# A decoder layer on one core: queries and keys stored in the layout of their products, and row additions moved off GpSimd

## The chip, the cores and the metric

The kernel runs on one core of a Trainium2 chip. The time is the device time of one execution in microseconds; the kernel before has a median of 1358.45 us over three runs (1357.38 to 1362.58). A profile of one further execution is the source of everything said about single instructions.

TensorE (PE) multiplies matrices, VectorE (DVE), ScalarE (ACT) and GpSimd (POOL) work on elements, and SyncE (SP) only issues transfers here. Each engine works through its own instructions in order and waits at the head of its queue when something is not ready.

## The reference

Four sequences of 1024 tokens with 256 features go through one decoder layer, with 64 context tokens for each sequence:

```python
x = x + attention(layernorm(x), W_qkv, b_qkv, W_out, b_out)   # 16 heads of 16, softmax(q k^T) / sqrt(256)
x = x + cross_attention(layernorm(x), ctx)                    # 16 heads of 16, 64 keys
x = x + ffn(layernorm(x))   # ternary W_fc to 1024, gelu, layernorm with w and b, ternary W_proj back
```

Everything is float32. Each of the three terms ends in a sum over features that is added to the rows of `x`; the attention's outputs have a bias row each (`b_out`, called `bo` in the kernel, and the cross attention's `xbo`), and the last layer norm's offset `ln_b` multiplied with `W_proj` gives another constant row, `yrow`.

## The kernel before

**Units.** Self-attention is worked in 16 units `u`, each one batch and four heads (`g`), all 1024 queries by 1024 keys. The queries and keys are kept as the sum of a high and a low part so that products in the faster float format lose nothing: `project(b, c)` computes, for one batch and eight heads at a time (128 padded features, 16 for each head), the high part on ScalarE and the low part on VectorE (tile `hl`, two parts by 512 tokens; the two lines that write `hl` are L369 and L370). It does so for the first half of the queries, both halves of the keys, then the second half of the queries: four pieces. Each piece is stored to DRAM (`kept_q`, `kept_k`, L375) by one transfer of 512 KB. Most transfers go through the helper at L62 on SP's queue; in the very first group three of the stores go on ScalarE's.

**Fetch.** `fetch(u)` reads the four heads of a unit back, two heads ("pair") to a tile of 128 partitions: for each head 16 rows of the queries' parts in the order high, high, low, low, and of the keys' parts in the order high, low, high, low. One product over these 64 rows then gives the sum of all four part products. Since DRAM holds each part once, a tile takes eight transfers of 16 rows: 64 KB each, and for unit 0, which is fetched by halves of the tokens, 32 KB each. Half of unit 0's key fetches are issued by ScalarE (L393). The fetches of unit u+1 are issued in the first two steps of unit u.

**A unit.** `maxima(u)` multiplies queries by keys in blocks of 128 queries by 512 keys and takes the exact row maxima on VectorE (L446); the maxima are negated and split in parts as well (`nm`, L455; `nm_s`, L458 and L459), turned (`mT`, L464), and used in the scores, which are computed again with keys on the partitions; ScalarE takes the exponentials (L911), and the weighted values are summed in `ps_acc`. A unit has 16 steps (two halves of the queries by eight blocks of keys). The maxima of unit u+1 run between the scores of unit u; for unit 0 the first 32 of them must come before anything else.

**What fills the gaps.** All other work (layer norm and projections of the next batches, values, `post(b)`) is written as generators on three lines (`due`, `later`, `aside`), and a step of a unit takes pieces from them as their due times demand. The order of TensorE's instructions and of the transfers on SP is the order written in the program. On VectorE, ScalarE and GpSimd a scheduler decides the order, save for some pinned layer norm instructions. A transfer also waits for the one eight transfers before it.

**post(b).** After a batch's attention: add the bias row `bo` to `x` (four additions of 128x512 a batch on GpSimd through `add_row`, L287 to L293), output projection added to `x` (L327), layer norm (`ln_stats` L241 and L242, `ln_normalised`: one instruction for each 256-feature row block, on ScalarE at L258 in the main part and on VectorE at L265 in the last stage), then add `xbo` to `x`, turn the normalised rows (`ln_transposed`, L279 and L281), and the cross attention. `post(3)` runs in the last stage.

**The last stage** is the feed-forward part, in eight half batches. `widen(i)` normalises, turns, multiplies to 1024 features, applies gelu and takes the statistics of the last layer norm; it also adds `yrow` to `x`. `narrow(i)` turns the 1024 features, scales them (L1060, and the low part `hl` on VectorE, L1061), multiplies back to 256, adds to `x` (L1077) and stores the output. A written order interleaves the `widen` and `narrow` of neighbouring halves, and puts pieces of `post(3)` between them. `state["split"]` is true in the main part and false here.

Of the kernel before, what the change touches and what calls it, by code (L numbers as in the profile page):

```python
# [30 lines left out]
def decoder_layer(ctx, tc, a, out):  # L31
# [240 lines left out]
    def ln_transposed(dst, xn, rest=None):  # L272

        def copy(tokens, r, sides, v):
            to = of_side(dst[:, :, tokens], r, sides)
            nc.scalar.copy(to, v)  # L279
            if rest is not None:  # L280
                nc.vector.tensor_tensor(  # L281
                    of_side(rest[:, :, tokens], r, sides), v, to.bitcast(F32), ALU.subtract
                )

        turned_tokens(copy, lambda c, k: xn[:, k, c * P : (c + 1) * P], xn.shape[1])

    def add_row(t, row, n=2):  # L287

        for t in range(t, t + n, 2):
            nc.gpsimd.tensor_tensor(  # L290
                xs(t, 2), xs(t, 2),
                row.rearrange("p (o d) -> p o d", o=1).to_broadcast([P, 2, E]), ALU.add,
            )  # L293
# [56 lines left out]

    def project(b, c):

        split_of[b, c] = [
            dram.tile([2, P, S], F32, tag=f"kept_{name}", name=f"kept_{name}", bufs=6) for name in "qk"
        ]
        first = (b, c) == (0, 0)

        for side, half in ((0, 0), (1, 0), (1, 1), (0, 1)):
            w, bias = (wq, wk)[side], bqk[("bq", "bk")[side]][:, c : c + 1]
            hl = main.tile([P, 2, 512], F32, tag="exp" if first and half else "hl", name="hl", bufs=4 if first and half else 2)  # L360
            width = 256 if state["split"] else 512
            for i0 in range(0, 512, width):
                yield "cols+"
                cols, part = slice(half * 512 + i0, half * 512 + i0 + width), slice(i0, i0 + width)
                pq = bank()[:, 0:width]
                product(
                    pq, [(w[:, i, c * P : (c + 1) * P], xnT_of[b][:, i, cols]) for i in range(2)]
                )
                nc.scalar.activation(hl[:, 0, part].bitcast(F32R), pq, AF.Identity, bias=bias)  # L369
                nc.vector.scalar_tensor_tensor(  # L370
                    hl[:, 1, part], pq, bias, hl[:, 0, part], ALU.add, ALU.subtract
                )
            cols = slice(half * 512, (half + 1) * 512)
            issue = nc.scalar.dma_start if first and (side or half) else dma
            issue(out=split_of[b, c][side][:, :, cols].rearrange("l p t -> p l t"), in_=hl)  # L375
            pieces_of[b, c] = pieces_of.get((b, c), 0) + 1

    def fetch(u):

        b, g = divmod(u, NG)  # L380
        pairs = qk_of[u] = []
        rest = []
        for pair in range(2):
            q = main.tile([P, S], F32R, tag="q", name="q", bufs=4)
            k = main.tile([P, S], F32R, tag="k", name="k", bufs=4)
            pairs.append((q, k))
            kept_q, kept_k = split_of[b, g // 2]
            f0 = 64 * (g % 2) + 32 * pair

            def parts(t, kept, order, n, cols, issue, f0=f0):  # L390
                for i, part in enumerate(order):
                    r, f = 64 * n + 16 * i, f0 + 16 * n
                    issue(out=t[r : r + 16, cols].bitcast(F32), in_=kept[part, f : f + 16, cols])  # L393

            if u:
                halves = (slice(0, S),)
            else:
                halves = (slice(0, 512), slice(512, S))
            for n in range(2):
                parts(q, kept_q, (0, 0, 1, 1), n, halves[0], dma)  # L400
            for cols in halves:
                for n in range(2):
                    parts(k, kept_k, (0, 1, 0, 1), n, cols, dma if u or n else nc.scalar.dma_start)
            for n in range(2):
                for cols in halves[1:]:
                    rest.append((parts, q, kept_q, (0, 0, 1, 1), n, cols, dma))
            if pair:
                for f, *args in rest:
                    f(*args)
            yield  # L410

    def values(b):
# [140 lines left out]
    def post(b):  # L553
        t0 = b * NT
        pairs = att_of.pop(b)
        yield "free"
        add_row(t0, bo, NT)

        def projected(src, w, first, n):

            for i in range(0, n, 4):
# [17 lines left out]
        for half in range(2):  # L579
# [1 line left out]
            xnT = post_pool.tile([P, 2, 512], F32, tag="xn2T", name="xn2T")  # L581
            yield "free"
            xn = ln_normalised(post_pool, mv, rs, h0, t0 + h0, 4)
            add_row(t0 + h0, xbo, 4)
            yield "rows"
            ln_transposed(xnT, xn)
            q2 = post_pool.tile([P, 2, 512], F32, tag="q2", name="q2")
            m = 256 if state["split"] else 512
            for i in range(0, 512, m):
# [324 lines left out]
    for u in range(NU):  # L914
        b, g = divmod(u, NG)
        due.end = aside.end = 2 * NT * NG * (b + 1)
        later.end = due.end - 2
        if b % 2 and g == 0:
            due.end = 2 * NT * (u + 1)
        if g == 0:  # L920
            if b == 0:
                later.add(context(), 6)
                later.add(value_bias(), 1)

            for n in ((1, 2), (), (3,), ())[b]:
                if n > 2:
                    load_x(n)
                due.add(ln1(n), 2)
                due.add(project(n, 0), 8)
                due.add(values(n), 8)  # L930
                if n == 1:
                    due.add(project(n, 1), 8)
            if b % 2:

                due.add(project(b // 2 + 2, 1), 8)
            if b == B - 1:
                load_x(0, view=x_kept, slot=1)
        if g == 1 and b == B - 1:
            aside.add(ternary("wfc", 2, HID), 10)
            aside.add(ternary("wproj", HID // P, E), 10)  # L940
            aside.add(bias_row(), 2)
        for step in range(2 * NT):
            half, kb = divmod(step, NT)
            if u == 1 and step == 2:
                load_x(2)
            if step < 2 and 0 < u < NU - 1:
                if step == 0:
                    while pieces_of.get(divmod((u + 1) // 2, NG // 2)) != 4:
                        due.step()
                    fetching = fetch(u + 1)  # L950
                next(fetching)
            next(loading, None)
            due.grow(2 * NT * u + step)
            later.grow(2 * NT * u + step)
            aside.grow(2 * NT * u + step)
            exps = [scores(u, half, kb, 0)]
            top()
            behind = 1 if later.credit >= 1.5 else 0
            if turning and begun[turning[0]] < slots[0]:
                fill("rows", behind)  # L960
                run(turning.popleft())
            elif urgent:
                fill("rows", behind)
                urgent.popleft()()
            else:
                fill("rows", 1)
            exps.append(scores(u, half, kb, 1))

            for _ in range(2 if u == 0 and step < 3 else 1):
                top()  # L970
            if pending is not None:
                if pending[2] == 0:
                    acc = ps["acc"]()
                weigh(*pending, acc)
            fill("cols", 2)
            pending = (u, half, kb, exps)
        if g == NG - 1:

            due.flush()
            aside.flush()  # L980
            later.flush()
    weigh(*pending, acc)
    while urgent:
        urgent.popleft()()
# [16 lines left out]
    def widen(i):  # L1001
# [3 lines left out]
        for t in range(0, NH, 2):  # L1005
            cols = slice(t * P, (t + 2) * P)
            xn = ln_normalised(ffn, mv3, rs3, t0 + t, t0 + t, 2)
            ln_transposed(xh[:, :, cols], xn, rest=xl[:, :, cols])
            add_row(t0 + t, yrow)
            if t == 0:  # L1010
                yield ""
        h = ffn.tile([P, NH, HID], F32, tag="h", name="h", bufs=2)
# [32 lines left out]
    def narrow(i):  # L1045
# [6 lines left out]
        for c in range(HID // P + 2):  # L1052
# [10 lines left out]
            if c >= 2:  # L1063
                for k, part in enumerate(parts[c - 2]):
                    for n in range(NH):


                        matmul(
                            py[:, n // 2, n % 2 * E : (n % 2 + 1) * E], lhsT=part[:, n * P : (n + 1) * P],
                            rhs=wproj[:, c - 2, :], start=c == 2 and k == 0 and n % 2 == 0,  # L1070
                            stop=c == HID // P + 1 and k == 1 and n % 2 == 1,
                        )
            if 0 < c < HID // P + 1:
                yield ""
        for n in range(2):
# [113 lines left out]
```

## Time and profile before

| | |
|---|---|
| median of the runs | 1358.45 us (1357.38 to 1362.58) |
| profiled execution | 1359.89 us, its span 1358.1 us |
| TensorE busy | 1282.7 us (94%) |
| VectorE busy | 1005.3 us (74%) |
| ScalarE busy | 896.6 us (66%) |
| GpSimd busy | 79.6 us (6%) |
| mean granted TensorE clock | 0.978 |
| HBM read / written | 46.81 MB / 24.12 MB |
| 240 + 240 fetches of 64 KB | issued on SP from 48.74 us on |
| 32 + 32 fetches of 32 KB | unit 0, 16 of them issued by ScalarE |
| 32 stores of 512 KB | 29 on SP, 3 on ScalarE |
| row additions on GpSimd, 128x512 | 16 `bo`, 16 `xbo`, 16 `yrow`, about 1.3 us each |

Times in the profile are microseconds from the start of the span unless marked ns. A row of a timeline has the start, the length, the engine, the line of the kernel, the operation, what it writes and reads, and how many such instructions stand in a row; in brackets how long the engine had been idle and what ended that. SPq and ACTq are the issuing of transfers by SP and ScalarE; an issue is short, and where a row of several is long, the engine stands in them waiting. PEld is TensorE's loading of weights, which overlaps its products. PEclk is the clock that TensorE was granted, as a share of full speed. DMA share is the mean busy share of the core's 16 transfer engines.

### The profile page before, as it was taken

What the parts mean: (1) busy time and instruction counts of PE and PEld (TensorE: products, weight loads), DVE (VectorE), ACT (ScalarE), POOL (GpSimd) and SP (SyncE); (2) the same over time, 40 slices, a digit from 0 to 9 for tenths busy, and PEclk for the clock granted to TensorE, in tenths of its full rate; (3) what the DMA queues carried; (4) which work ended last, traced back from release to release, by engine and by line L of the source; (5) the groups of instructions that cost most, each with busy time, mean ns of one, the idle gap of its engine ahead of it and who ended that gap; (6) DMA issues with size and microseconds to landing.
All of it is one profiled execution on the core that took longest, in us unless ns stands there. A gap on an engine that the chain in (4) does not pass through costs nothing.

```text
span 1358.1 us, 27680 instructions
## 1 busy us (share of the span) xinstructions
PE 1282.7 (94%) x11000; PEld 719.2 (53%) x11000; DVE 1005.3 (74%) x2110; ACT 896.6 (66%) x1654; POOL 79.6 (6%) x86
## 2 busy tenths in 40 slices
PE   5889999999999999989999999999999988999987
PEld 2345445545554554444545545545455466776777
DVE  4788877767878877778877767878889357565665
ACT  1277676766677667777676676686766747474765
POOL 4000000022010000011000000010000012000000
PEclk9689999999999999999999999999999989999989
DMA  5431321302020201221111102212210010100000
GB/s 171 133 120 48 109 62 65 95 32 79 33 79 1 63 27 38 71 56 43 53 46 50 45 19 83 75 61 65 63 33 1 2 63 0 51 12 32 1 32 31
DMA packets 46576, 72.72 MB, mean 54 GB/s; under 512 B 11536, under 2 KB 28176, under 8 KB 46448
## 3 DMA queue, kind: packets, MB, share of 16 engines
q1 hardware_dynamic: 44976, 68.47, 16.7%
q10 hardware_dynamic: 1328, 2.10, 0.5%
q8 instruction: 87, 1.43, 0.4%
q0 software_dynamic: 144, 0.39, 0.2%
q14 instruction: 41, 0.34, 0.1%
HBM read 46.81 MB, written 24.12 MB: 52 GB/s over the span
## 4 chain that ended last, share of the span: by engine, by line
PE 75%; DVE 15%; ACT 7%; DMA 2%; issue 1%; SPq 0%; DVEq 0%; ACTq 0%
PE ps_ring L57 44%; PE ps_acc L57 15%; PE ps_wide L57 8%; DVE mx L446 7%; PE ps_misc L57 3%; PE ps_misc L60 2%; ACT exp L911 2%; PE ps_ring L60 2%; DVE nm L605 2%; ACT xn L258 1%; DMA x<-in_x 1%; DVE bn L241 1%; DVE xn L265 1%; DMA q<-kept_q 1%; ACT ex L638 1%
## 5 line engine op out<-in xcount | busy, mean ns | idle before, releaser
L446 DVE TENSOR_REDUCE mx<-ps_ring 128x1 f32<-128x512 f32 x1024 | 646.7, 681 | 154.7 <-PE ps_ring L57 153.7
L911 ACT ACTIVATE exp<-ps_ring 128x512 f32<-128x512 f32 x1024 | 549.3, 607 | 182.6 <-PE ps_ring L57 179.1
L57 PE MATMUL ps_ring<-q,k 64*128 64x512 f32 x1024 | 280.4, 474 | 8.3 <-ACT exp L911 5.9
L57 PE MATMUL ps_ring<-k,q 64*128 64x512 f32 x1024 | 265.3, 428 | 15.6 <-DMA k<-kept_k 4.7
L57 PE MATMUL ps_acc<-exp,v_sb 128*32 128x512 f32 x2048 | 274.5, 608 | 0.0
L57 PE MATMUL ps_ring<-mT,sel 64*128 64x512 f32 x1024 | 233.1, 401 | 0.2 <-ACT mT L464 0.2
L57 PEld LDWEIGHTS ps_ring<-q,k 64*128 64x128 f32 x1024 | 115.9, 185 | 199.0 <-ACT exp L911 68.2
L57 PEld LDWEIGHTS ps_ring<-k,q 64*128 64x128 f32 x1024 | 126.1, 187 | 98.5 <-ACT exp L911 40.9
L57 PEld LDWEIGHTS ps_ring<-mT,sel 64*128 64x128 f32 x1024 | 108.4, 187 | 6.2 <-ACT mT L464 0.7
L57 PEld LDWEIGHTS ps_acc<-exp,v_sb 128*32 128x32 f32 x2048 | 40.5, 108 | 67.2 <-issue 65.4
L1029 DVE BATCH_NORM_STATS2 bnh<-h 128x6 f32<-128x512 f32 x64 | 41.1, 679 | 34.1 <-ACT h L1026 34.0
L1026 ACT ACTIVATE h<-ps_wide 128x1024 f32<-128x1024 f32 x32 | 32.7, 1025 | 42.0 <-PE ps_wide L57 41.9
L1061 DVE SCALAR_TENSOR_TENSOR hl<-ps_misc,lnw,hT 128x512 fp32r<-128x512 f32 x64 | 46.4, 733 | 18.2 <-ACT hT L1060 18.2
L57 PE MATMUL ps_wide<-wfc,xl 128*128 128x512 f32 x128 | 56.6, 443 | 1.9 <-DVE xl L281 1.8
L57 PE MATMUL ps_wide<-wproj,hl 128*128 128x256 f32 x256 | 46.2, 303 | 12.5 <-DVE hl L1061 12.4
L57 PE MATMUL ps_wide<-wfc,xh 128*128 128x512 f32 x128 | 54.2, 423 | 0.0
L1060 ACT ACTIVATE hT<-ps_misc,lnw 128x512 fp32r<-128x512 f32 x64 | 42.6, 686 | 16.3 <-PE ps_misc L60 16.3
L241 DVE BATCH_NORM_STATS2 bn<-x 128x6 f32<-128x256 f32 x96 | 38.9, 416 | 6.6 <-DMA x<-in_x 5.0
L57 PEld LDWEIGHTS ps_wide<-wproj,hl 128*128 128x128 f32 x256 | 34.9, 192 | 16.2 <-DVE hl L1061 14.7
L290 POOL TENSOR_TENSOR x<-x,xbo 128x512 f32<-128x512 f32 x16 | 20.5, 1288 | 367.3 <-ACT xn L258 358.2
L57 PE MATMUL ps_wide<-wproj,hT 128*128 128x256 f32 x256 | 41.4, 285 | 0.0
L60 PE MATMUL ps_misc<-ident,h 128*128 128x128 f32 x256 | 37.4, 274 | 1.0 <-ACT ex L638 0.7
(166 smaller groups left out, 1436.8 us busy)
## 6 DMA issues: line engine op xcount, KB each, us to landing
q<-kept_q SPq DMA_DIRECT2D x240, 64.0 KB
k<-kept_k SPq DMA_DIRECT2D x240, 64.0 KB
kept_q<-hl SPq DMA_DIRECT2D x15, 512.0 KB
kept_k<-hl SPq DMA_DIRECT2D x14, 512.0 KB
out<-x SPq DMA_DIRECT2D x16, 256.0 KB
x<-in_x SPq DMA_DIRECT2D x3, 1024.0 KB
x_kept<-x SPq DMA_DIRECT2D x3, 1024.0 KB
x<-x_kept SPq DMA_DIRECT2D x3, 1024.0 KB
```

The lines of the kernel that those rows point to most:

```text
L57: ordered(nc.tensor.matmul(*args, **kwargs))
L60: ordered(nc.tensor.transpose(*args))
L241: pinned(nc.vector.bn_stats(out=st, in_=xs(t)[:, 0, :]))
L258: nc.scalar.activation(xn[:, k, :], xs(t + k)[:, 0, :], AF.Identity, bias=nmr[:, k : k + 1], scale=rs[:, i + k : i + k + 1],)
L290: nc.gpsimd.tensor_tensor(xs(t, 2), xs(t, 2), row.rearrange("p (o d) -> p o d", o=1).to_broadcast([P, 2, E]), ALU.add,)
L446: nc.vector.tensor_reduce(mx[:, t, 2 * pair + n : 2 * pair + n + 1, kh], pm, AX.X, ALU.max)
L605: nc.vector.tensor_reduce(nm[:, t, s, :], pm[s].rearrange("p (h k) -> p h k", k=SK), AX.X, ALU.max, negate=True,)
L911: nc.scalar.activation(ex[:, n, :], pe[n], AF.Exp)
L1026: nc.scalar.activation(h[:, t, :], ph.rearrange("p a f -> p (a f)"), AF.Gelu)
L1029: nc.vector.bn_stats(out=st[:, half, :], in_=h[:, t, half * 512 : (half + 1) * 512])
L1060: nc.scalar.activation(hT, pt, AF.Copy, scale=w)
L1061: nc.vector.scalar_tensor_tensor(hl, pt, w, hT.bitcast(F32), ALU.mult, ALU.subtract)
```

## The change

- The kept tiles get the shape [8 heads, 4 parts, 16 features, 1024 tokens], with the parts in the order in which the products take them: each part is in DRAM twice. A piece is stored by four transfers of 256 KB, one for each of the four part positions.
- A tile of a pair is then a contiguous block of 128 rows and is fetched by one transfer of 512 KB; in unit 0 by two of 256 KB (the second half of the queries after everything else, as before). All fetches are issued on SP. SP issues 245 transfers instead of 618, ScalarE 12 instead of 19.
- `bo` is added in the ninth of the sixteen steps of a batch's last unit (for batch 0, after that unit) instead of at the head of `post`, whose first yield goes.
- `xbo` is added after the normalised rows have been turned instead of before.
- `yrow` is added in `narrow`, with its columns 4 and 6, instead of in `widen`.
- `add_row` uses VectorE in the last stage: that takes the 16 `yrow` additions and the four `xbo` additions of batch 3 there. The other 28 stay on GpSimd.

The scheduler's order of VectorE and ScalarE moves with this. Of these moves three bear on what follows: the first `bn_stats` of batch 1's layer norm stands right behind the first `nm`, ahead of `nm_s`; batch 1's normalisations stand singly among the exponentials; and the statistics of batch 2 stand earlier among the maxima.

```diff
     def add_row(t, row, n=2):
 
+        engine = nc.gpsimd if state["split"] else nc.vector
         for t in range(t, t + n, 2):
-            nc.gpsimd.tensor_tensor(
+            engine.tensor_tensor(
                 xs(t, 2), xs(t, 2),
                 row.rearrange("p (o d) -> p o d", o=1).to_broadcast([P, 2, E]), ALU.add,
             )
...
         split_of[b, c] = [
-            dram.tile([2, P, S], F32, tag=f"kept_{name}", name=f"kept_{name}", bufs=6) for name in "qk"
+            dram.tile([8, 4, D, S], F32, tag=f"kept_{name}", name=f"kept_{name}", bufs=6)
+            for name in "qk"
         ]
...
             issue = nc.scalar.dma_start if first and (side or half) else dma
-            issue(out=split_of[b, c][side][:, :, cols].rearrange("l p t -> p l t"), in_=hl)
+            for i, part in enumerate(((0, 0, 1, 1), (0, 1, 0, 1))[side]):
+                issue(out=split_of[b, c][side][:, i, :, cols], in_=hl[:, part, :])
...
-            kept_q, kept_k = split_of[b, g // 2]
-            f0 = 64 * (g % 2) + 32 * pair
-
-            def parts(t, kept, order, n, cols, issue, f0=f0):
-                for i, part in enumerate(order):
-                    r, f = 64 * n + 16 * i, f0 + 16 * n
-                    issue(out=t[r : r + 16, cols].bitcast(F32), in_=kept[part, f : f + 16, cols])
...
+            h = 4 * (g % 2) + 2 * pair
+            kept_q, kept_k = (
+                t[h : h + 2].rearrange("h i f t -> (h i f) t") for t in split_of[b, g // 2]
+            )
+            halves = (slice(0, 512), slice(512, S)) if u == 0 else (slice(0, S),)
+            dma(out=q[:, halves[0]].bitcast(F32), in_=kept_q[:, halves[0]])
             for cols in halves:
-                for n in range(2):
-                    parts(k, kept_k, (0, 1, 0, 1), n, cols, dma if u or n else nc.scalar.dma_start)
+                dma(out=k[:, cols].bitcast(F32), in_=kept_k[:, cols])
+            if u == 0:
+                rest.append((q, kept_q))
             if pair:
+                for q, kept_q in rest:
+                    dma(out=q[:, 512:S].bitcast(F32), in_=kept_q[:, 512:S])
             yield
...
     def post(b):
         t0 = b * NT
         pairs = att_of.pop(b)
-        yield "free"
-        add_row(t0, bo, NT)
...
             xn = ln_normalised(post_pool, mv, rs, h0, t0 + h0, 4)
-            add_row(t0 + h0, xbo, 4)
             yield "rows"
             ln_transposed(xnT, xn)
+            add_row(t0 + h0, xbo, 4)
...
             next(loading, None)
+            if b and g == NG - 1 and step == NT:
+
+                add_row(b * NT, bo, NT)
...
             later.flush()
+            if b == 0:
+
+                add_row(0, bo, NT)
...
             ln_transposed(xh[:, :, cols], xn, rest=xl[:, :, cols])
-            add_row(t0 + t, yrow)
...
+            if c in (4, 6):
+                add_row(t0 + c - 4, yrow)
             if 0 < c < HID // P + 1:
                 yield ""
```

## The prediction

> **What bounds the kernel now.** I read the page's busy line, slices and chain first, then the issues of SP and ACT in the opening, then stretches of 10 us, and the last stage's groups at the end.
>
> ```profile
> PE 1282.7 (94%) x11000; PEld 719.2 (53%) x11000; DVE 1005.3 (74%) x2110; ACT 896.6 (66%) x1654; POOL 79.6 (6%) x86
> PE   5889999999999999989999999999999988999987
> PEclk9689999999999999999999999999999989999989
> PE 75%; DVE 15%; ACT 7%; DMA 2%; issue 1%; SPq 0%; DVEq 0%; ACTq 0%
> ```
>
> TensorE is the bound at 94%, so a gain can only come from the 75 us in which it is idle, or runs at a lower clock. The slices place them: the first three, a dip in the middle (560 to 600 us), and the last eight (the last stage, from 1095 us). From 107 to 200 us TensorE is busy 92.36 of 93.00 us, so transfers made cheaper there are worth nothing.
>
> SP's issues, then ACT's, in the opening (start, length, engine, line, what it writes and reads, count, idle before):
>
> ```profile
> 17.06 0.37 SPq L63 DMA_DIRECT2D kept_q<-hl  x1
> 19.86 6.98 SPq L63 DMA_DIRECT2D q<-kept_q  x8
> 27.62 4.68 SPq L63 DMA_DIRECT2D k<-kept_k  x8
> 48.74 5.64 SPq L63 DMA_DIRECT2D q<-kept_q  x8
> 65.53 0.42 SPq L63 DMA_DIRECT2D x<-in_x  x1
> ```
>
> ```profile
> 26.90 5.12 ACTq L393 DMA_DIRECT2D k<-kept_k  x6
> 29.65 5.93 ACTq L393 DMA_DIRECT2D k<-kept_k  x11
> 35.68 0.84 ACT L369 ACTIVATE hl<-ps_ring,bq_c 128x256 fp32r<-128x256 f32 x2 [10.82 <-DMA k<-kept_k]
> ```
>
> A store of 512 KB is issued at 17.06 and its reader at 19.86: 2.8 us. Then some 0.45 us goes for each small fetch, and ACT issues fetches until 35.6 while its `hl` work, which holds PSUM banks, stands behind them. The first row maximum starts at 31.80, the 32nd ends at 60.24, the scores start at 61.0. The next batch's x load is issued last, at 65.53.
>
> The stretches (length, PE, PEld, DVE, ACT, POOL busy with counts, granted clock, DMA share, GB/s):
>
> ```profile
> 17.00:20.00 3.00, 2.13 (x12) 1.33 (x11) 0.79 (x2) 1.65 (x3) 3.00 (x4) 1.00 0.54 211
> 50.00:60.00 10.00, 7.09 (x74) 2.98 (x66) 10.00 (x18) 1.49 (x4) 0.00 (x0) 0.97 0.61 175
> 80.00:90.00 10.00, 7.33 (x72) 3.49 (x71) 8.71 (x29) 5.62 (x11) 0.52 (x3) 1.00 0.36 113
> 90.00:100.00 10.00, 7.73 (x42) 3.33 (x44) 6.94 (x15) 9.64 (x19) 0.99 (x6) 0.66 0.00 0
> ```
>
> From 50 to 60 DVE is full: maxima at some 0.61 us each are that stage's floor. From 80 to 100 TensorE is idle 4.9 us and the clock falls to 0.66, about 2 us more: the layer norm of batch 1 stands in ACT's and DVE's way in one block. That block costs 7 us.
>
> **The opening: the transfers.** Removed: 16 fetches of 32 KB from ACT, and on SP eight issues a tensor become one (two or three halves in unit 0). Added: each store becomes four of 256 KB, 1 MB a piece for 512 KB, since every part is stored twice. Only unit 0 feels the fetches, which elsewhere land under a full TensorE.
>
> What such a store costs no row shows, because its DRAM side is now `[8,16,512]` (heads, features, tokens), where the old one began with 128. By the row, 512 KB moved in 1.35 us (18.0 to 19.4 us, 389 GB/s over 16 DMA engines, 24.3 GB/s each), so a doubled piece would take 2.7 us. The Trainium skill, "DMA: Bandwidth & Descriptors", section "Why a DMA increments its semaphore by 16 and not by 1", says that a DMA runs on the largest number of engines up to 16 that divides the slowest dimension of both sides: here 8, always the lowest-numbered. Then each 256 KB takes 1.35 us on eight engines and a piece 5.4 us, fourfold. No run here shows it. I take the rule, since nothing in the row has an outer dimension of 8, and keep the row's value for the low end.
>
> By the rule, on engines 0 to 7 (24.3 GB/s each): they start at 17.45; unit 0's four pieces 4 × 5.4 = 21.6; its eight fetches of 256 KB at 0.68, 5.4; two pieces of the next four groups 10.8; unit 1's fetches of 2 MB, 5.4; the x load of 1 MB, 2.7. Sum 45.9, plus some 1.5 us idle while SP waits for a store: x lands at about 65.5. The first keys' fetch, behind stores of the two queues, lands at 31.4, so the first maximum starts where it did; ACT now waits for store lanes till about 34 instead of 35.6. From the second keys' fetch (37.4) DVE runs on: 24 × 0.61 = 14.6, plus `hl` work, and the 32nd maximum ends at about 53.
>
> Then comes what is late next. In the built order of DVE, the first `bn` of batch 1's layer norm stands directly between `nm` and the `nm_s` that the scores need. It waits for x. Behind it are `nm_s`, the transposes, `mT`, every exp. So DVE stands from 53 to 65.5 and scores start at about 66.5, against 61.0: +5.5 us.
>
> In return, the block at 80 to 100 is gone: statistics follow at 66 (eight pairs at some 0.4 and 0.1 us), and ACT's eight normalisations stand singly among the exps. What remains: two table loads of 1.28 us on ACT and 3.3 us on DVE, side by side, at the start of scores; I take 2 left of 7: −5. (Batch 2's norm, spread in this way, lies between 107 and 200 us, where TensorE idled 0.6 us in all.)
>
> By the row's 2.7 us a piece the same sum ends otherwise: first maximum at 28, no pause before it, 32nd at 50, x landed at 48: scores at 51, −10, and the norm −3.5.
>
> **The steady part.** `hl` has two buffers; a piece written before the second-last one's stores are read would hold ACT and its exps. Stores are issued at 129.34, 146.82 and 149.15: two back is 19.8 us, against about 7.5 for four issues and 5.4 of data, so nothing. Batch 2's statistics are hoisted from 159 to some 141 us, about when its x lands: the load moves up from 146.3 to 132, behind 2 MB of fetches: 5.4, then 2.7 us: +1. The x load of batch 3, before 571.57 to 577.86 among small fetches (TensorE idle 4.7 us around it), comes through sooner: −1.5. The bo rows move from the head of `post` to a point before it and stay on POOL: 16 × 1.29 beside a full TensorE, 0; nothing else waits in POOL's queue there, and the 12 xbo rows left on it have until the projection after them. With its yield gone `post` starts one fill earlier, which moves work and adds none.
>
> **The last stage.** Four xbo and 16 yrow additions go from POOL to DVE, set right behind the normalisations by the built order. These groups (busy, mean ns, idle before) and one stretch tell the price, then DVE's own timeline:
>
> ```profile
> L290 POOL TENSOR_TENSOR x<-x,yrow 128x512 f32<-128x512 f32 x16 | 20.8, 1302 | 213.3 <-DVE xn L265 142.2 <-issue 68.5 <-DVE rsh L248 2.3
> L1077 DVE TENSOR_TENSOR x<-x,ps_wide 128x512 f32<-128x512 f32 x16 | 10.3, 682 | 9.9 <-PE ps_wide L57 9.9
> ```
>
> ```profile
> 1120.00:1140.00 20.00, 14.99 (x84) 12.55 (x83) 19.31 (x43) 13.53 (x16) 7.28 (x6) 0.95 0.00 0
> ```
>
> ```profile
> 1131.53 3.94 DVE L265 TENSOR_SCALAR xn<-x,mv,rs 128x256 f32<-128x256 f32 x6
> ```
>
> Added: 20 × 0.68 (nearest row: same shape, one side in PSUM) = 13.6 us of DVE. Removed: DVE's normalisations take 0.38 us alone and about 0.35 pipelined, but six took 3.94 us beside POOL's additions; that is 1.85 too much, and with five other such places (0.9, 1.0, 1.1, 1.0, 1.0) about 7 us goes. DVE is the bound only from 1120 to 1140 (19.31 of 20): six additions 4.1, less 2.85 relief, +1.2. In the other stretches it idles 25 to 45% and TensorE is busy; 14 additions 9.5 less 4.1, mostly hidden: +0.8. Together +2. Bounds: −7 (relief felt, additions hidden) to +10.8 (all additions felt, relief only in that stretch).
>
> **Sum.** +5.5 − 5 + 1 − 1.5 + 2 = +2 on the profiled 1359.89 (span 1358.1): 1361.9. The median of the runs, 1358.45, is 1.4 below the profiled one, so 1360.5; I say 1360.
>
> **Rivals.**
> - *Stores run on 16 engines* (the row holds, or contention is less). For it: 389 GB/s in the trace. Against: the rule. −10 − 3.5 + 1 − 1.5 + 2 = −12: 1346.
> - *The last stage decides, slower.* The additions stand ahead of `hl` or `xl`, for which TensorE already waits 12.4 us at `hl`: 10.8 in place of 2: 1369. It decides from seven uncovered additions more than I count (7 × 0.68 = 4.8). Against: DVE idles a third of most stretches.
> - *x is later or the norm isn't absorbed.* If the start costs 5.5 and the norm saves only 2, 1363.5.
> - *The transfers don't matter*: opening as before, hidden by DVE's maxima; 1358.45 + 1.5 = 1360. Only the traces tell it from my case.
>
> **How the numbers follow.** Mine 0.55; sixteen engines 0.13; last stage 0.15; norm not absorbed 0.12; transfers hidden 0.05. A measurement here tells from no change about 0.5%: 1351.7 to 1365.2. Faster: 0.12 from sixteen engines, 0.07 from mine (relief, or less waiting for x): 0.19. Slower: 0.15, 0.05 of the norm's, and 0.12 of mine (terms of 5 us each, all rough): 0.32. Within: 0.49. The range reaches to both: 1346 to 1370; mine alone 1353 to 1367.
>
> **What would show it.** Right: kept stores that land some 1.35 us after one another with DMA share near 0.5; DVE waiting about 10 us for x's load ahead of `nm_s`; scores from 66 us; no block at 80 to 100; normalisations at 0.38 us and DVE above 75% in the last stage. Wrong: share near 1 during stores, scores at about 51; or TensorE waiting for `hl` much over 12.4 us in the last stage.

## The result, and the profile after

The changed kernel takes 1374.24 us (median of six runs, 1373.14 to 1377.56) against 1360.73 us of the kernel before in the same comparison: a ratio of 1.0105, with a 95% interval of 1.0086 to 1.0124. It is slower by 13.5 us, and lies 4 us above the upper end of the predicted range. The profiled execution has a span of 1372.5 us, 14.4 more than the one before.

The page of the changed kernel, its busy line, slices and chain:

```profile
PE 1280.1 (93%) x11000; PEld 714.2 (52%) x11000; DVE 1012.7 (74%) x2130; ACT 896.9 (65%) x1654; POOL 53.4 (4%) x66
PE   4689899989999999989999999998999998999988
PEclk9789999999999999999999999999999999999999
PE 40%; DVE 10%; ACT 4%; DMA 1%; issue 1%; SPq 0%; DVEq 0%; ACTq 0%
```

TensorE's work is the same to 0.2%; its idle time has grown by 17 us (92.4 against 75.4), and the slices show that most of this lies in the first tenth of the span. Sums over the whole span don't say more. What does is to find the same instruction in both traces and take the difference of its starts. The exponentials (1024 of them, in the same order in both) and the additions of the last stage serve as marks; a change of the shift between two marks is what that stretch gained or lost:

| mark | before, us | after, us | shift | the stretch lost (+) or gained (−) | predicted |
|---|---|---|---|---|---|
| exponential 1 | 63.7 | 75.8 | +12.1 | opening +12.1 | +5.5 |
| 33 | 100.4 | 108.6 | +8.2 | layer norm of batch 1 −3.9 | −5 |
| 97 | 160.8 | 179.4 | +18.6 | layer norm of batch 2 +10.4 | +1 |
| 257 | 317.2 | 337.3 | +20.1 | +1.5: −3.6 up to exponential 221, then a jump of +5.5 at 300 us | 0 |
| 545 | 608.9 | 625.4 | +16.5 | around batch 3's x load −3.6 | −1.5 |
| 833 | 908.0 | 924.1 | +16.1 | −0.4 | 0 |
| 865 | 939.5 | 962.2 | +22.7 | ternary weights +6.6 | none |
| 993 | 1067.7 | 1091.4 | +23.7 | +1.0 | 0 |
| addition 15 of 16 at the end (`x<-x,ps_wide`) | 1353.3 | 1367.9 | +14.6 | last stage −9.1 | +2 |

SP's and ACT's timelines of the changed kernel in the opening:

```profile
16.73 3.40 SPq L63 DMA_DIRECT2D kept_q<-hl  x4
28.76 0.35 SPq L63 DMA_DIRECT2D q<-kept_q  x1
32.88 8.53 SPq L63 DMA_DIRECT2D k<-kept_k  x2
61.70 0.43 SPq L63 DMA_DIRECT2D x<-in_x  x1
```

```profile
19.54 6.38 ACTq L379 DMA_DIRECT2D kept_k<-hl  x4
25.96 0.58 ACT L279 COPY xnT<-ps_ring 128x512 f32<-128x512 f32 x1 [5.97 <-issue]
30.42 0.69 ACT L372 ACTIVATE hl<-ps_ring,bk_c 128x512 fp32r<-128x512 f32 x1 [3.87 <-PE ps_ring L57]
```

Between the first store's issue and the fetch that reads it lie 12.0 us; before it was 2.8. And ScalarE stands in its four stores for 6.4 us with the second half of the turned rows behind them, so that the second half of the keys comes 9.4 us later (30.42; before, 21.00). The first maximum starts at 40.81 instead of 31.80 (before, then after):

```profile
31.80 0.69 DVE L446 TENSOR_REDUCE mx<-ps_ring 128x1 f32<-128x512 f32 x1 [6.15 <-PE ps_ring L57]
```

```profile
40.81 1.29 DVE L440 TENSOR_REDUCE mx<-ps_ring 128x1 f32<-128x512 f32 x2 [4.29 <-PE ps_ring L57]
```

DVE's timeline behind the 32 maxima:

```profile
64.95 0.19 DVE L449 TENSOR_REDUCE nm<-mx 128x16 f32<-128x32 f32 x1
72.05 0.43 DVE L241 BATCH_NORM_STATS2 bn<-x 128x6 f32<-128x256 f32 x1 [6.91 <-DMA x<-in_x]
72.40 0.16 DVE L452 CAST nm_s<-nm 128x16 fp32r<-128x16 f32 x1
...
155.58 0.43 DVE L241 BATCH_NORM_STATS2 bn<-x 128x6 f32<-128x256 f32 x1 [6.73 <-DMA x<-in_x]
```

The wait of the prediction is there, ahead of `nm_s`, and it comes a second time for batch 2. Two more waits for late transfers follow, on ScalarE for stores of `hl` and on DVE for a load (timelines of each):

```profile
299.09 0.47 ACT L372 ACTIVATE hl<-ps_ring,bq_c 128x256 fp32r<-128x256 f32 x1 [4.02 <-DMA kept_k<-hl]
```

```profile
940.01 0.69 DVE L742 TENSOR_REDUCE part<-raw 128x1 f32<-128x512 f32 x1 [5.90 <-DMA raw<-in_wfc]
```

Each of the last three (batch 2, 300 us and 940 us) costs more than TensorE's idle time. TensorE stood for 5.81, 3.98 and 3.95 us, and its granted clock was then 0.50 for about 5 us more after it had work again, which takes some 2.4 us of work each time. Together that comes near the losses of 10.4, 5.5 and 6.6 us in the table. The stall of batch 2, and the stretches behind the stall at 300 us (the third column from the end is the clock):

```profile
156.44 0.79 PE L57 MATMUL ps_ring<-k,q 64*128 64x512 f32 x1 [5.81 <-DVE hl L373]
```

```profile
302.00:304.00 2.00, 2.00 (x20) 0.59 (x12) 0.22 (x1) 0.00 (x0) 0.00 (x0) 0.50 0.00 0
306.00:308.00 2.00, 2.00 (x24) 0.86 (x25) 2.00 (x4) 1.86 (x5) 0.00 (x0) 1.00 0.43 79
```

What the stores do to the transfer engines shows in stretches of the changed kernel (the last two columns are the DMA share and GB/s):

```profile
17.00:30.00 13.00, 6.06 (x15) 2.79 (x14) 3.41 (x12) 1.75 (x3) 3.98 (x5) 0.80 0.55 165
56.00:60.00 4.00, 3.87 (x42) 1.58 (x40) 4.00 (x7) 0.74 (x2) 0.00 (x0) 1.00 0.55 206
64.00:72.00 8.00, 0.00 (x0) 0.00 (x0) 1.10 (x3) 0.00 (x0) 0.00 (x0) 0.61 0.83 309
```

While only stores run (56 to 60), the share is about a half at 206 GB/s. From 64 to 72 TensorE does nothing at all.

The last stage, by groups of DVE instructions (the normalisations before, then two groups of the changed kernel):

```profile
L265 DVE TENSOR_SCALAR xn<-x,mv,rs 128x256 f32<-128x256 f32 x40 | 20.2, 548 | 2.6 <-PE ps_misc L60 2.0 <-PE ps_acc L57 0.6
```

```profile
L265 DVE TENSOR_SCALAR xn<-x,mv,rs 128x256 f32<-128x256 f32 x40 | 14.8, 406 | 0.6 <-PE ps_acc L57 0.6
L291 DVE TENSOR_TENSOR x<-x,yrow 128x512 f32<-128x512 f32 x16 | 10.6, 683 | 0.0
```

An addition costs 0.68 us on DVE, as the nearest row had it, and the normalisations have come down from 548 to 406 ns on average.

### The profile page after: what moved, and what is told of

It is laid out like the page before. It is cut to its first block, busy times and chain, and to the rows that moved or that the text cites. A ratio compares the mean times of both kernels' runs of the same rounds, so it can differ in the third digit from the quotient of the medians.

```text
span 1372.5 us, 27267 instructions
## 1 busy us (share of the span) xinstructions
PE 1280.1 (93%) x11000; PEld 714.2 (52%) x11000; DVE 1012.7 (74%) x2130; ACT 896.9 (65%) x1654; POOL 53.4 (4%) x66
## 4 chain that ended last, share of the span: by engine, by line
PE 40%; DVE 10%; ACT 4%; DMA 1%; issue 1%; SPq 0%; DVEq 0%; ACTq 0%
PE ps_ring L57 18%; PE ps_wide L57 8%; PE ps_acc L57 7%; DVE mx L440 4%; PE ps_misc L57 3%; PE ps_misc L60 2%; DVE nm L596 2%; ACT exp L902 1%; PE ps_ring L60 1%; DMA raw<-in_wproj 1%; DMA raw<-in_wfc 1%; DVE h L1033 0%; DVE xl L281 0%; ACT xn L258 0%; DVE hl L1057 0%
## 5 line engine op out<-in xcount | busy, mean ns | idle before, releaser
L57 PEld LDWEIGHTS ps_ring<-k,q 64*128 64x128 f32 x1024 | 123.2, 187 | 107.5 <-ACT exp L902 47.1
L57 PE MATMUL ps_wide<-wproj,hl 128*128 128x256 f32 x256 | 46.8, 306 | 10.6 <-DVE hl L1057 10.5
L57 PE MATMUL ps_ring<-xnT,wk 128*32 128x256 f32 (+1 forms) x456 | 36.7, 398 | 6.9 <-ACT xnT L279 6.9
L373 DVE SCALAR_TENSOR_TENSOR hl<-ps_ring,bq_c,hl 128x256 f32<-128x256 f32 (+1 forms) x30 | 14.9, 500 | 37.8 <-ACT hl L372 37.8
L57 PEld LDWEIGHTS ps_wide<-wproj,hl 128*128 128x128 f32 x256 | 35.3, 194 | 14.3 <-DVE hl L1057 12.6
L372 ACT ACTIVATE hl<-ps_ring,bq_c 128x256 fp32r<-128x256 f32 (+1 forms) x30 | 14.7, 495 | 42.2 <-PE ps_ring L57 33.0
```

The lines of the kernel that those rows point to most:

```text
L57: ordered(nc.tensor.matmul(*args, **kwargs))
L373: nc.vector.scalar_tensor_tensor(hl[:, 1, part], pq, bias, hl[:, 0, part], ALU.add, ALU.subtract)
```

## The experiments

Twelve kernels were run. Each ratio is against runs of the kernel before on the same chip. These kernels ran on three chips: the kernel before took 1359.68 us beside the `only` kernels and `rows16_adds`, 1361.15 beside the `early` and `once` kernels and 1360.51 beside the last four. A difference of a few microseconds between kernels of two groups is better read from the ratios.

| kernel | us | ratio (95%) |
|---|---|---|
| stores on 8 engines, additions of the change (the changed kernel) | 1374.24 | 1.0105 (1.0086 to 1.0124) |
| `dma8_only`: its transfers, additions as before | 1382.64 | 1.0170 (1.0149 to 1.0191) |
| `adds_only`: its additions, transfers as before | 1354.45 | 0.9958 (0.9942 to 0.9975) |
| `rows16_adds`: other row order, additions of the change | 1342.18 | 0.9874 (0.9853 to 0.9896) |
| `rows16_only`: other row order, additions as before | 1351.39 | 0.9932 (0.9914 to 0.9949) |
| `early_8`: the changed kernel, `x` loaded before the stores | 1367.81 | 1.0052 (1.0038 to 1.0067) |
| `early_16`: `rows16_adds`, `x` loaded before the stores | 1340.11 | 0.9844 (0.9825 to 0.9863) |
| `once`: each part stored once and read twice, additions of the change | 1336.51 | 0.9821 (0.9800 to 0.9842) |
| `once_early`: the same, `x` loaded before the stores | 1335.84 | 0.9817 (0.9801 to 0.9833) |
| `four_engines`: the changed kernel, each store cut in two | 1405.36 | 1.0330 (1.0311 to 1.0349) |
| `dve_rows`: the kernel before, its last-stage additions on DVE | 1355.75 | 0.9967 (0.9955 to 0.9980) |
| `moved_rows`: the kernel before, its additions moved, all on GpSimd | 1359.79 | 1.0000 (0.9991 to 1.0008) |
| `no_rows`: `adds_only` without the 20 additions of the last stage | 1352.56 | 0.9944 (0.9931 to 0.9956) |

### How many engines a store takes

The theory is that the store is slow because its DRAM side begins with a dimension of 8; the rivals are that the doubled bytes are the cost, or the order of the layer norm's instructions. A product over 64 rows doesn't care about the order of the rows, as long as queries and keys agree. So the row order head, feature, part, token serves as well as head, part, feature, token; with it a store is 128 rows at one stride, and nothing else changes:

```diff
-            dram.tile([8, 4, D, S], F32, tag=f"kept_{name}", name=f"kept_{name}", bufs=6)
+            dram.tile([8, D, 4, S], F32, tag=f"kept_{name}", name=f"kept_{name}", bufs=6)
...
-                issue(out=split_of[b, c][side][:, i, :, cols], in_=hl[:, part, :])
+                issue(
+                    out=split_of[b, c][side][:, :, i, cols].rearrange("h f t -> (h f) t"), in_=hl[:, part, :]
+                )
...
-                t[h : h + 2].rearrange("h i f t -> (h i f) t") for t in split_of[b, g // 2]
+                t[h : h + 2].rearrange("h f i t -> (h f i) t") for t in split_of[b, g // 2]
```

> The changed kernel, but with DRAM rows ordered head, feature, part, token, so that a store's DRAM side is 128 rows with one stride, as its SBUF side is; bytes, number of transfers and everything else stay. If the eight engines are the cause: 16 completions a store instead of 8, DMA share near 1 while stores run, about 0.65 us for 256 KB instead of 1.29, scores from about 51 us instead of 73, DVE's waits for the x loads of 6.9 and 6.7 us and ScalarE's wait of 4.0 us for a kept store gone, and a time of about 1338 us. If the doubled bytes are the cause, whatever engines carry them, some 1365 to 1374. If the order of the layer norm's instructions is the cause, 1365 to 1374 as well, with DVE still waiting ahead of nm_s.

It took 1342.18 us: 32 us less than the changed kernel, with the same bytes and the same number of transfers. The stretch of the opening, of this kernel:

```profile
17.00:30.00 13.00, 9.67 (x74) 4.70 (x76) 4.70 (x14) 3.59 (x6) 3.35 (x5) 0.87 0.97 305
```

The share is 0.97 where it was 0.55. All 2130 instructions of DVE stand in the changed kernel's order, with the first `bn` between `nm` and `nm_s`, so the order alone is not the cause. But the waits for x are shorter rather than gone (2.14 us ahead of `nm_s`, 2.30 us at batch 2): scores start at 55.8, not at 51, and the two waits together are about the 4 us by which it missed 1338.

> The change's stores and fetches alone; all row additions where the kernel before has them, on GpSimd. If the last stage gained from the additions (the shift between the traces falls from 23.7 to 14.6 us there), this is about 9 us slower than the changed kernel, near 1383 us. If the last stage's gain is only slack taken up again after a late start, it is as the changed kernel, 1374.

> Stores and fetches with rows ordered head, feature, part, token, row additions as before. If the engines and the additions are two separate effects: about 9 us above the run that has both, near 1347 us. If the transfers' gain is given back in the last stage, nearer to 1360.

> The row additions alone; stores and fetches as before. If the additions gain 9 us in the last stage: about 1351 us. As I had predicted for the last stage (+2): 1362. If the gain is slack: 1360.

These three, with `rows16_adds`, the changed kernel and the one before, take the two halves of the change apart. `dma8_only` came out as expected; `adds_only` and `rows16_only` each took some 4 us longer than expected, but nearer to that than to the other case. With the additions as before, the eight-engine stores cost 23.0 us (1382.64 − 1359.68) and the sixteen-engine stores gain 8.3. The additions gain 5.2 us beside the old stores and 9.2 beside the sixteen-engine ones; beside the eight-engine ones the two medians differ by 8.4. They are not slack taken up again: they gain without any late start. By the marks the last stage itself gains 8.8 us in `adds_only`, 9.0 in `rows16_adds` and 9.1 in the changed kernel; `adds_only` gains less in all because it is 2.2 us behind the kernel before when the last stage begins. Nor does the last stage gain from the transfers beside the sixteen-engine stores (−0.1 in `rows16_only`); in `dma8_only` it takes back 2.7 us.

The other direction of the same cause is a store cut in two, of four heads each, with twice as many transfers:

```diff
-                issue(out=split_of[b, c][side][:, i, :, cols], in_=hl[:, part, :])
+                for h in (0, 4):
+                    issue(
+                        out=split_of[b, c][side][h : h + 4, i, :, cols],
+                        in_=hl[16 * h : 16 * h + 64, part, :],
+                    )
```

> The changed kernel with each store cut into two of four heads, so that the slowest dimension of the DRAM side is 4. By the rule: four completions a store, 128 KB in about 1.29 us, a piece 10.3 us, DMA share near 0.25 while only stores run; with six pieces ahead of batch 1's x it lands near 95 us, scores start about 20 us later than in the changed kernel, and the time is 1395 us or more. If the number of engines follows from the bytes or the partitions, 1374 to 1380.

1405.36 us. A stretch of this kernel in which only stores run:

```profile
28.00:32.00 4.00, 0.00 (x0) 0.00 (x0) 0.00 (x0) 0.00 (x0) 0.00 (x0) 0.50 0.26 102
```

The share is a quarter. The trace also records the completions of each transfer, one for every engine that took part. Set side by side, with the time between one landing and the next while stores follow each other:

| store | bytes | completions | landings apart | GB/s |
|---|---|---|---|---|
| before, [128 rows] | 512 KB | 16 | | 389 |
| row order head, feature, part | 256 KB | 16 | 0.64 to 0.65 us | 405 |
| the change, [8, 16 rows] | 256 KB | 8 and one more | 1.28 to 1.29 us | 204 |
| cut in two, [4, 16 rows] | 128 KB | 4 and one more | 1.28 to 1.29 us | 102 |

(GB/s is bytes by the time between landings; in the first row, by the 1.35 us that the prediction read.) The one more comes about 1 us after the issue, before any data: the section that the prediction cites (the Trainium skill, "DMA: Bandwidth & Descriptors") says that the issuer at once writes the missing count itself, which agrees. The scores of `four_engines` start only 4 us behind the changed kernel's, not 20: here the scheduler put `nm_s` ahead of the layer norm, and DVE waits for x later, 10.12 us before 102.58. The expected 20 us are there by the 33rd exponential, which is 17 us behind the changed kernel's. The place of the wait was wrong, its size nearly right.

### Whether the late x is the stall

```diff
     wv = load_w("wv", E, late=True)
+    load_x(1)
...
     run(fetch(1))
-    load_x(1)
+    load_x(2)
...
-            if u == 1 and step == 2:
-                load_x(2)
```

> The changed kernel with its eight-engine stores; only the x loads move: batch 1's to right behind the load of wv, before any store, and batch 2's to where batch 1's was. If it is the late x that turns slow stores into a stall: DVE no longer waits ahead of nm_s, scores start at 66 us instead of 73 (the 32nd maximum ends at 65), the wait at 149 us goes too, and the time is about 1374 - 7 - 9 = 1358 us. If TensorE is held by the stores themselves, whose data still come when they come, the two waits are replaced by others and it stays above 1368.

1367.81 us: 6.4 us less than the changed kernel (7 by the ratios), where I had expected 16, and at the rival's bound of 1368. DVE's timeline:

```profile
63.73 0.17 DVE L454 TENSOR_TENSOR nm_s<-nm,nm_s 128x16 f32<-128x16 f32 x1
70.81 0.75 DVE L242 BATCH_NORM_STATS2 bn<-x 128x6 f32<-128x256 f32 x2 [6.90 <-DMA x<-in_x]
```

`nm_s` no longer waits, and the first exponential starts at 66.7 instead of 75.8. But the scheduler moved batch 2's layer norm into the freed place, right behind `nm_s`, and it waits as long for the next x: the shift from the kernel before goes from +3.0 at the first exponential to +8.1 at the 65th. The batch 2 stall at 97 is gone (+7.9 there, where the changed kernel has +18.6), and ScalarE waits for kept stores twice, for 9.5 us in all. So the late x was the stall ahead of `nm_s`, but the rival's description, waits that are replaced by others, fits this run as well as mine: while the stores are slow, taking one stall away hands it to the next reader of a late transfer.

> The rows ordered head, feature, part, token and the x loads moved as in the other run. In the run with these rows DVE still waits for x ahead of nm_s (TensorE idle 6.5 us) and 5.3 us are lost at batch 2's statistics. If x is the cause of both: 1342 - 6 - 5 = 1331 us. If not: 1340.

1340.11 us, 2.1 less than with the x loads where they were (4 by the ratios, whose intervals overlap), and not 11. With sixteen engines DVE's waits were short already, as said above; and with x loaded first the maxima end 2.0 us later (54.47, where `rows16_adds` has 52.46). My expectation had read the whole of TensorE's gap of 6.5 us as the wait for x.

### Whether the bytes matter as well

The doubling can be undone without giving up the large fetch. The rows of one head and feature lie side by side in DRAM, once each, and the transfer reads them twice by a stride of zero: the queries' tile in one transfer of 512 KB, the keys' tile in two, each to every second row.

```diff
+            dram.tile([8, D, 2, S], F32, tag=f"kept_{name}", name=f"kept_{name}", bufs=6)
...
+            issue(out=split_of[b, c][side][:, :, :, cols].rearrange("h f l t -> (h f) l t"), in_=hl)
...
+            def twice(t, kept, inner, cols):
+                n = cols.stop - cols.start
+                if inner:
+                    src = kept[:, :, cols].rearrange("r l (o t) -> r l o t", o=1)
+                    dma(out=t[:, cols].bitcast(F32), in_=src.to_broadcast([32, 2, 2, n]))
+                else:
+                    for part in range(2):
+                        src = kept[:, part, cols].rearrange("r (o t) -> r o t", o=1)
+                        dma(out=t[part:P:2, cols].bitcast(F32), in_=src.to_broadcast([32, 2, n]))
```

> Every part is in DRAM once again, in rows of head, feature, part, token: one store of 512 KB a piece; the fetch of a query tile is one transfer that reads each row twice, that of a key tile two transfers of 64 rows. The x loads stay where the change has them. If the bytes of the stores still delay x (4 MB less is stored by then, at some 390 GB/s 10 us, of which x gains about 5): scores at some 51 instead of 56 us, less of a wait at batch 2, about 1335 us. If reading a row twice costs as much as storing it twice: 1342.

1336.51 us. DVE's timeline of this kernel:

```profile
52.80 0.18 DVE L459 TENSOR_REDUCE nm<-mx 128x16 f32<-128x32 f32 x1
53.02 0.24 DVE L462 CAST nm_s<-nm 128x16 fp32r<-128x16 f32 x1
53.30 0.18 DVE L463 TENSOR_TENSOR nm_s<-nm,nm_s 128x16 f32<-128x16 f32 x1
53.39 0.75 DVE L241 BATCH_NORM_STATS2 bn<-x 128x6 f32<-128x256 f32 x2
```

x has landed at 49.15, before the maxima end, and nothing waits. Two things differ from `rows16_adds` at once, the bytes and the scheduler's order (here `nm_s` stands first), so the 5.7 us between them (7 by the ratios) are not divided further. Scores start at 53.6 and not at 51, because the maxima end at 52.8: they are the floor now.

> Both: parts stored once and x loaded before the stores. If the waits for x are then gone in both ways, it gains little on either alone: about 1330 us, and within 3 us of the run that has the rows of head, feature, part, token and the early x.

1335.84 us, the same as `once` within the spread of either, and 4.3 us below `early_16`. This is the best version found, 1.8% below the kernel before.

### What the additions gain

> The kernel before with one edit: row additions in the last stage on VectorE instead of GpSimd, at the places where they were. If what the additions gain is that GpSimd's additions no longer stretch VectorE's normalisations: these at 0.40 us instead of 0.55 on average, and about 1355 us, as the run with all of the additions' edits (1354.45). If it is the moved places: 1360.

> The kernel before with the additions moved to the places of the change, all still on GpSimd. If the stretching is the cause: about 1360 us, normalisations at 0.5 us or more. If the moved places are the cause (post one fill earlier, xbo and yrow off the way of what reads x): 1355.

`dve_rows` is the kernel before with one line of `add_row` changed; `moved_rows` has all of the change's moves, on GpSimd. 1355.75 and 1359.79 us: the engine gains 4.8 us, the moves by themselves nothing. The timeline of DVE in `moved_rows`, and the group in `dve_rows` (last stage):

```profile
1122.90 7.73 DVE L265 TENSOR_SCALAR xn<-x,mv,rs 128x256 f32<-128x256 f32 x9
```

```profile
L265 DVE TENSOR_SCALAR xn<-x,mv,rs 128x256 f32<-128x256 f32 x40 | 15.0, 404 | 1.8 <-PE ps_misc L60 1.2 <-PE ps_acc L57 0.6
```

Nine normalisations beside GpSimd's additions took 0.86 us each; without GpSimd the average is 0.40. In `moved_rows` 21 of the 40 stand beside an addition, 13 in the kernel before, and their sum grows from 20.2 to 22.6 us without a longer time. So the moved places may gain something that the longer normalisations take back; that would fit the last stage's gain by the marks, which is 4.5 us with the engine alone, 0.8 with the moves alone and 8.8 with both. No run shows it apart.

> The additions' edits, and the 20 row additions of the last stage left out altogether (16 of yrow, four of xbo, so those rows are missing from the output). It prices the additions where they now stand: if VectorE hides them, 1354 us as with them; if they are felt in full, 13.2 us less, 1341.

1352.56 us, 1.9 us less than with the additions in place, and the two intervals overlap; the additions are 13.2 us of DVE's time (10.6 of `yrow`, 2.6 of `xbo`). Nearly all of it is hidden. (By the marks `no_rows` even gains less in the last stage than `adds_only`, 6.2 against 8.8 us; its lead lies in the main part. Why is open.)

## Why the prediction was wrong, point by point

The mechanism, stores on eight engines that make x late, was the right one; terms of the sum were not. By the marks above, +2 was predicted and +14.6 measured. Three terms for late transfers were too small: the landing of x in the opening (6.6 us), that of batch 2's x (9.4) and that of the ternary weights, which had no term (6.6). One erred the other way: the last stage was put at +2 and gave −9.1. That the total missed by 12.6 us and not by some 24 is luck.

- *Stores on eight engines.* Right, and by the rule rather than by the row: 1.29 us for 256 KB was measured, 1.35 predicted. The rule, and not the trace, was all I leaned on, while the trace of before already had it: the loads of `bq_c`, whose DRAM side begins with 4, have four completions and one more, the 512 KB stores sixteen. No row of the profile shows that; the records of completions do.
- *The opening, +5.5 predicted, +12.1 measured.* The step that failed is the sum that ends in "x lands at about 65.5". (Its terms give 17.45 + 45.9 + 1.5 = 64.9.) x landed at 72.03; landings here are the last completion that the trace records for a transfer. By the sum unit 0's stores and fetches were through at about 46; they were through at 53.54. What stands behind them, eight stores, unit 1's fetches and x, then took 18.5 us, where 18.9 was summed. Part of the 7.6 us can be placed: the first store landed at 20.87 instead of 18.8; between the third and the fourth (24.30 and 28.62) came the three 128 KB rows that GpSimd loads (they land between 25.1 and 27.6), for which the sum had no term; and ScalarE and SP paused between their issues.
- *The start of the maxima, in the same stretch.* "The first maximum starts where it did", and the 32nd ends at about 53, failed too: 40.81 and 64.9. I had the first keys' fetch land at 31.4; it landed at 39.92. The eight stores ahead of it were through at 32.81 only, and the fetch then took 7.04 us: eight of its sixteen completions stand between 35.38 and 36.14, the other eight between 38.18 and 39.92, beside the next stores. And ScalarE, held for 6.4 us in its issues, passed the second keys' product on 9.4 us later; the prediction counted ScalarE's hold only for the `hl` work behind the second piece. But DVE stood waiting for x behind the maxima, so their lateness only shortened that wait, to 6.9 us instead of 12.5. The wait ahead of `nm_s` was forecast rightly, and it is x's landing that set the scores.
- *The layer norm of batch 1, −5 predicted, −3.9 measured.* Right.
- *Batch 2, +1 predicted, +10.4 measured.* The step "the load moves up to 132" failed. SP could issue the fetches ahead of it only at 140.5, behind eight stores with SP's waits for earlier transfers between them, and x's load at 144.06. It landed after 11.5 us, behind 2 MB of fetches and the tail of the stores, at 155.55: only 2.4 us later than in the kernel before (153.13). There its reader stood at 159.23; here the statistics had been hoisted to some 149 us, and the DVE work behind them fed TensorE, which then stood for 5.8 us and ran at a clock of 0.50 for 5 more. The prediction had no term for that clock. Some 3.6 of the 10.4 us come back by exponential 221.
- *The two buffers of `hl`, nothing predicted.* Failed: I took the pieces' spacing from the kernel before and asked for two pieces back. A piece's four stores now last from 290.52 to 298.98 us, 8.5 and not 7.5, and ScalarE's wait ended 0.1 us after the last of them, on the semaphores of these four stores: it waited for the piece just before. Why not for the one before that, with two buffers, is open.
- *The ternary weights, no term at all, +6.6.* In the changed order DVE reads the weights' rows 8.6 us after SP issues their load (931.41 to 940.01), behind a whole fetch of 2 MB in the queue; before, it came 14.7 us after (924.75 to 939.42). DVE stood for 5.9 us and TensorE for 3.95. I looked for readers of late loads only in the two layer norms.
- *Batch 3's x, −1.5 predicted, −3.6 measured.* Right in sign.
- *The last stage, +2 predicted, −9.1 measured.* The price (0.68 us) was right, and the relief nearly: 5.4 us show in the normalisations' sum (20.2 to 14.8 us), where about 7 was summed. The step that failed is what hides: I let most of the relief be hidden, and put the part of the additions that shows above it. `no_rows` shows that no more than some 2 us of the additions are felt, and `dve_rows` that 4.8 us are gained with the additions at their old places. What the moved places add to that was not taken apart, so the cause of the other 4 us is open. DVE was to be above 75% busy here; it was 69% (175.7 of 254 us from 1118 us on).

Of the rivals, "x is later or the norm isn't absorbed" named the place that failed, though what it summed was a norm that saves less: x was 6.5 us later, and the norm was absorbed (−3.9). "Stores run on 16 engines" describes `rows16_adds`, where 1346 was worked out and 1342 measured. "The last stage decides, slower" has the wrong sign. "The transfers don't matter" is refuted by the 23 us that the stores and fetches cost without the additions.

## What to carry to other kernels

When you lay out a tensor in DRAM, look at the slowest dimension of the transfers that write it, and not only at their bytes and their number: the same bytes, stored as 8 heads or as 128 rows, made some 32 us of difference here. Another order of the rows was free to choose, because the product sums over them. When stores become slower, list every reader of a later transfer in the queue, and check in the built order what stands behind it; a reader that has been moved up turns a late load into a stall of everything behind it on its engine, and TensorE then lost clock on top of the idle time. And where one engine's work stretches another's, price both sides: taking GpSimd's additions away gained more than it cost DVE to do them.

## What the runs showed of the hardware

- The rate follows the engines: 405, 204 and 102 GB/s for stores on 16, 8 and 4 of them, so about 25.4 GB/s each, with no gain for the few from the idleness of the rest. Stores of two queues share the same few: in `four_engines` SP and ScalarE issue stores in turn, and they land at 28.07, 28.76, 30.64, 31.32, 33.23, 33.90, 35.79 and 36.47 us, two in 2.57 us, no faster than one queue alone lands them (one in 1.28).
- A kernel whose fetches read each row of DRAM twice by a stride of zero is no slower than one that stores each row twice (1336.51 against 1342.18 us), and 16 completions are recorded for such a fetch.
- GpSimd's additions on 128x512 make DVE's normalisations (128x256) up to 1.38 us long in the kernel before, 0.85 on average where an addition stands beside them and 0.40 where none does; with the additions on DVE none is longer than 0.42.
- After TensorE had stood for 4.0 to 5.8 us (before 156.44, 300.10 and 941.35 us in the changed kernel), its granted clock was 0.50 for about 5 us after it had work again. Eight products into `ps_acc` took 1.93 us at 300.92 and 1.06 at 291.79.
